# A Perceiver stack: quantised feed-forward by tiles, expert rows turned one tile ahead, one more expert tile by way of DRAM

## The chip, the cores and the metric

The kernel runs on one core of a Trainium2 chip (trn2). The metric is device time in microseconds for one execution. Three runs of the kernel before took 2646.3, 2650.88 and 2655.88 us, median 2650.88.

## What is computed

The reference is a stack of four Perceiver layers on `x` of 2 x 256 tokens by 256, with a context of 2 x 4096 by 256. Each layer has a cross-attention or a convolution over the context, an attention or state-space block, and a feed-forward; each is added to `x` after a layer norm. All is fp32 but for the layers quantised by definition. Three feed-forwards matter here.

Layer 0, a ternary-weight feed-forward with activations rounded to 8 bits:

```python
def _act_quant(x):
    scale = 127.0 / jnp.clip(jnp.max(jnp.abs(x), axis=-1, keepdims=True), 1e-05)
    xq = jnp.clip(jnp.round(x * scale), -128.0, 127.0) / scale
    return x + jax.lax.stop_gradient(xq - x)
def _bitlinear(x, w):
    return jnp.einsum('bsi,oi->bso', _act_quant(x), _weight_quant(w))
gate = jax.nn.silu(_bitlinear(x, w_gate))      # 256 -> 1024
up = _bitlinear(x, w_up)
return _bitlinear(gate * up, w_down)           # 1024 -> 256
```

Layer 2, a shared SwiGLU expert and the two best of eight SwiGLU experts (256 -> 512 -> 256) for each token, weighted:

```python
topw, topi = jax.lax.top_k(probs, TOP_K)       # of 8, TOP_K = 2
topw = jax.nn.softmax(topw, axis=-1)
eout = jnp.einsum('etf,efd->etd', jax.nn.silu(gate) * up, e_down)
spec = jnp.einsum('etd,te->td', eout, combine)
```

Layer 3, the best of eight ReLU experts (256 -> 1024 -> 256) for each token:

```python
top1 = jnp.argmax(logits, axis=-1)
for e in range(n_experts):
    h = jax.nn.relu(xf @ w1[e].T + b1[e])
    y = h @ w2[e].T + b2[e]
    out = out + jnp.where((top1 == e)[:, None], y, 0)
```

## The kernel before

The 512 tokens are NT = 4 tiles of 128 rows, one row to a partition; KC = 2 is the number of 128-wide chunks of the 256 features. The layers run one after the other. Matmuls all go through the helper `mm` (line 358). PSUM banks are dealt out in rotation under three names, `mm`, `tr` and `acc` (3, 3 and 2 banks in the stages told of here). A framework schedules the instructions and sets the semaphores; `in_order` (line 337) pins the order in which the engines named take the instructions written inside it, to the order of the text.

**Layer-0 feed-forward** (`l0_ffn`, line 908). Everything is done for all four tiles before the next step begins. `act_quant` (line 892) takes the row maxima of a whole tensor in one instruction (L896), forms the step and its inverse in four small ones (L897 to L901), and rounds each tile in three passes on DVE: scale and add ROUND (12582912, which leaves a rounded integer in the low bits, L903), subtract ROUND and clip below (L904), clip above (L905). `to_T` (line 426) turns the result on PE (L434) and copies the banks to bf16 by turns on ACT (L330) and DVE (L332). For each tile t and each half j of the 1024 hidden columns, PE makes the gate and up products, ACT the SiLU (L929), DVE the product with the up half (L930) into `h`. Then `h` is rounded as a whole by `act_quant`, turned by `to_T`, and multiplied by the down weights; L941 scales and adds the residual.

**Experts** (`l2_ffn`, line 1671, and `l3_ffn`, line 2391). Tokens are sorted by expert into n tiles of 128 rows (15 in layer 2, 11 in layer 3), each tile of one expert. The sorted rows are written to DRAM by eight (layer 3: four) indirect DMAs (L1867) and loaded back as `rows` (L1877). One unit j is one tile. Its `front` loads the expert's weights by number (`of_expert`, line 2012, on the SP queue, three buffers to each weight), turns its 128 rows (`turn_chosen` for the first tiles, straight from the tokens, `turn_rows`, line 2030, for the rest: two transposes L2033, then on DVE L2041 in layer 2, L2038 in layer 3), makes the hidden products and their nonlinearity (L1737 on ACT and L1738 on DVE in layer 2; L2447 on DVE and L2445 on ACT by turns in layer 3). Its `back` multiplies by the down weights and copies the answer (`keep_rows`, line 2043, L2045 on ACT).

Answers return to the tokens in two ways. Tiles under `kept` (11 in layer 2, 9 in layer 3) are written to DRAM `ys` by the ACT queue (L2048); when unit kept-1 has written, `fetch_rows` (line 2002) gathers each token's row by indirect DMAs of GpSimd (L2006), eight in layer 2, four in layer 3; `add` adds them, weighted, at the end (L1785, L2469). The other tiles come back by matmul: `ways_back` (line 1922) builds for each a one-hot weighted matrix `way` (L1939 and L1942 on DVE, L1943 on GpSimd; layer 3 L1936), after turning the row numbers and weights once with `on_all` (L1917, L1919), and `bring_back` (line 1946) multiplies and adds it (L1952).

`experts_in_turn` (line 1964) sets the order: front(j), then back(j-1), then the bring-back of an earlier tile if one waits, then two steps of `ways`. From unit 3 on the order of PE, DVE and ACT is pinned by `in_order`:

```python
for j in range(straight, kept):
    got = unit(j)[0]()
    back_of(j - 1, waiting)
    waiting = got
    for _ in range(2):
        next(ways, None)
```

Of the kernel before, what the change touches and what calls it, by code (L numbers as in the profile page):

```python
# [11 lines left out]
F32 = mybir.dt.float32  # L12
BF16 = mybir.dt.bfloat16
# [255 lines left out]
class Perceiver:  # L269
# [619 lines left out]
            self.ternary[name] = q, mean  # L889
            yield  # L890

    def act_quant(self, x):

        nc = self.nc
        step = self.sm.tile([P, NT], F32, name="step", tag="step")
        nc.vector.tensor_reduce(step, x, AX.X, ALU.max, apply_absolute_value=True)  # L896
        nc.vector.tensor_scalar_max(step, step, 1e-5)  # L897
        inv = self.sm.tile([P, NT], F32, name="sinv", tag="sinv")
        nc.vector.reciprocal(inv, step)
        nc.vector.tensor_scalar_mul(inv, inv, 127.0)  # L900
        nc.vector.tensor_scalar_mul(step, step, 1.0 / 127.0)  # L901
        for t in range(NT):
            nc.vector.tensor_scalar(x[:, t, :], x[:, t, :], inv[:, t : t + 1], ROUND, ALU.mult, ALU.add)  # L903
            nc.vector.tensor_scalar(x[:, t, :], x[:, t, :], ROUND, -128.0, ALU.subtract, ALU.max)  # L904
            nc.vector.tensor_scalar_min(x[:, t, :], x[:, t, :], 127.0)  # L905
        return step

    def l0_ffn(self, x):
        nc = self.nc
        with self.tc.tile_pool(name="l0f", bufs=1) as pool, self.tc.tile_pool(name="l0f2", bufs=3) as p2:  # L910
            wg, mg = self.ternary["l0f_wg"]
            wu, mu = self.ternary["l0f_wu"]
            wd, md = self.ternary["l0f_wd"]
            xn = self.layernorm(x)
            sx = self.act_quant(xn)

            xT = self.to_T(xn, pool, "xqT", dtype=BF16)
            sg = self.sm.tile([P, NT], F32, name="sg", tag="sg")
            nc.vector.tensor_scalar_mul(sg, sx, mg)
            su = self.sm.tile([P, NT], F32, name="su", tag="su")  # L920
            nc.vector.tensor_scalar_mul(su, sx, mu)
            h = pool.tile([P, NT, 1024], F32, name="h")
            for t in range(NT):
                for j in range(2):
                    pg, pu = self.bank([P, 512]), self.bank([P, 512])
                    self.mm(pg, [(xT[:, k, ts(t, P)], wg[:, k, ts(j, 512)]) for k in range(KC)])
                    self.mm(pu, [(xT[:, k, ts(t, P)], wu[:, k, ts(j, 512)]) for k in range(KC)])
                    g = p2.tile([P, 512], F32, name="gate")
                    nc.scalar.activation(g, pg, AF.Silu, scale=sg[:, t : t + 1])  # L929
                    nc.vector.scalar_tensor_tensor(  # L930
                        h[:, t, ts(j, 512)], pu, su[:, t : t + 1], g, ALU.mult, ALU.mult
                    )
            sh = self.act_quant(h)
            hT = self.to_T(h, pool, "hqT", dtype=BF16)
            sd = self.sm.tile([P, NT], F32, name="sd", tag="sd")
            nc.vector.tensor_scalar_mul(sd, sh, md)
            y = self.xp.tile([P, NT, D], F32, name="xres", tag="xres")
            for t in range(NT):
                ps = self.bank([P, D])
                self.mm(ps, [(hT[:, k, ts(t, P)], wd[:, k, :]) for k in range(8)])  # L940
                nc.vector.scalar_tensor_tensor(y[:, t, :], ps, sd[:, t : t + 1], x[:, t, :], ALU.mult, ALU.add)  # L941
            return y


# [726 lines left out]
    def l2_ffn(self, x):  # L1671
        nc = self.nc
        T = NT * P
        with ExitStack() as s:
# [17 lines left out]
            router = self.weight("l2f_router")  # L1692
            ids = pool.tile([P, 8], F32, name="ids")
            nc.gpsimd.iota(ids, [[1, 8]], base=0, channel_multiplier=0, allow_small_or_imprecise_dtypes=True)
            n, straight, kept = 15, 2, 11
            xs = self.cleared_rows(pool, n)
            along, below = self.places(pool, n)
            lg = self.bank([P, NT, 8])
# [52 lines left out]
            ys = self.rows_in_dram("ys", kept)  # L1751

            def unit(j):
                def front():
                    gu, down = self.of_expert(pool, experts, j, ("l2f_gu", 1), ("l2f_down", 1))
                    hT = p3.tile([P, KC, P], F32, name="rowsT", tag="rowsT")
                    if j < straight:
                        self.turn_chosen(pool, hT, h2, ats, along, j, "norm2")
                    else:
                        self.turn_rows(hT, rows, j, "norm2")  # L1760
                    return expert(gu, down, hT, P, "e"), down

                def back(got):
                    aT, down = got
                    ps = self.acc([P, D])
                    self.mm(ps, [(aT[:, c, :], down[:, c, :]) for c in range(4)])
                    return self.keep_rows(p3, ys, j, ps, kept)

                return front, back

            held = [self.held(pool, i, at, kept) for i, at in enumerate(ats)]

# [191 lines left out]
    def experts_in_turn(self, unit, n, kept, gather, ways, way, y):  # L1964


        e = mybir.EngineType
        done = []

        def back_of(j, got):  # L1970
            one = unit(j)[1](got)
            while done:
                at, answers = done.pop(0)
                self.bring_back(y, way[at], answers)
            if one is not None:
                done.append((j, one))

        waiting, straight = None, 3
        for j in range(straight):
            got = unit(j)[0]()  # L1980
            if waiting is not None:
                back_of(j - 1, waiting)
            waiting = got
        with self.in_order(e.PE, e.DVE, e.Activation):
            for j in range(straight, kept):
                got = unit(j)[0]()
                back_of(j - 1, waiting)
                waiting = got
                for _ in range(2):
                    next(ways, None)  # L1990
            for j in range(kept, n):
                got = unit(j)[0]()
                back_of(j - 1, waiting)
                if j == kept:
                    add = gather()
                waiting = got
            back_of(n - 1, waiting)
            add()
            at, answers = done.pop(0)
            self.bring_back(y, way[at], answers)  # L2000

    def fetch_rows(self, pool, slots, ys):
        got = [pool.tile([P, NT, D], F32, name="got", tag="got", bufs=2) for _ in slots]
        for t in range(NT):
            for g, slot in zip(got, slots):
                self.nc.gpsimd.indirect_dma_start(  # L2006
                    out=g[:, t, :], out_offset=None,
                    in_=ys, in_offset=bass.IndirectOffsetOnAxis(ap=slot[:, t : t + 1], axis=0),
                )
        return got  # L2010
# [380 lines left out]
    def l3_ffn(self, x):  # L2391
        nc = self.nc
        with self.tc.tile_pool(name="l3f", bufs=1) as pool, self.tc.tile_pool(name="l3f3", bufs=3) as p3:
# [32 lines left out]
            ys = self.rows_in_dram("ys", kept)  # L2426

            def unit(j):
                def front():
                    w1, w2 = self.of_expert(pool, experts, j, ("l3f_w1", 0), ("l3f_w2", 0))  # L2430
                    bias = w1[:, KC * 1024 :]
                    w1 = w1[:, : KC * 1024].rearrange("p (k n) -> p k n", k=KC)
                    rT = p3.tile([P, KC, P], F32, name="rowsT", tag="rowsT")
                    if j < straight:
                        self.turn_chosen(pool, rT, xn, ats, along, j)
                    else:
                        self.turn_rows(rT, rows, j)
                    hT = p3.tile([P, 8, P], F32, name="hT", tag="hT")
# [19 lines left out]
                return front, back  # L2458

            yes, slot = self.held(pool, 0, ats[0], kept)  # L2460
            way = {}
# [94 lines left out]
```

## Time and profile before

The profiled execution took 2652.49 us. Times are microseconds from the start of its span; the clock is the granted share of TensorE's full clock.

| What | Value |
|---|---|
| profiled execution | 2652.49 us |
| its span, first to last instruction | 2650.7 us |
| mean granted clock | 0.953 |
| layer-0 feed-forward: first maximum (L896) to end of the last residual add (L941) | 224.0 to 262.6 |
| layer-2 experts: first front to the end of the last add (L1952) | 1825.1 to 1938.2 |
| time from one front to the next, units 9 to 12 of layer 2 | 6.26 to 6.27 us |
| layer-3 experts: first front to the end of the last add (L1952) | 2553.2 to 2646.8 |
| time from one front to the next, units 5 to 9 of layer 3 | 8.03 to 8.05 us |
| DMA share and rate in layer 2, 1851 to 1901 | 0.76, 264 GB/s |
| DMA share and rate in layer 3, 2558 to 2573 | 1.02, 411 GB/s |

A row of the timeline gives start, duration, engine (PE matmul, PEld its weight load, DVE, ACT, POOL for GpSimd, SPq and ACTq for DMA issues), line, operation, `out<-in`, shape and count, and in brackets the engine's idle time before it and what ended that. Where rows of one operation follow each other they stand as one, with a count. An fp32 matmul has two records to one instruction of the program.

### The profile page before, as it was taken

The page shows a single profiled execution, that of the slowest core. Times are in us where ns is not written, and L with a number is a line of the kernel's source. Part 1 is how long each engine was busy: PE and PEld are TensorE (multiplying, and loading weights), DVE is VectorE, ACT ScalarE, POOL GpSimd, SP SyncE. Part 2 cuts the span into 40 slices and gives each one's busy share as a digit, 9 for nine tenths or more (in the row PEclk, how much of TensorE's full clock was granted, in tenths as well). Part 3 has the DMA queues.
Part 4 walks back from the last instruction along what each step waited for, and adds up shares of the span by engine and source line. Part 5 has one row for each costly group of instructions (what it writes and reads, how often), then busy time and mean ns, then how long its engine had stood idle before and what let it go on. Part 6 is the DMA issues. An engine that isn't in the chain of part 4 may idle for free. (4 is left out here: it accounts for less than half of the span.)

```text
span 2650.7 us, 45617 instructions
## 1 busy us (share of the span) xinstructions
PE 2498.6 (94%) x17708; PEld 1668.9 (63%) x17709; DVE 1720.2 (65%) x3191; ACT 1346.6 (51%) x2545; POOL 921.6 (35%) x865
## 2 busy tenths in 40 slices
PE   8986999999999999999899988899889999999888
PEld 6853566666666676676533555557745666665677
DVE  5566577777777777777669655444257888854632
ACT  3323566666666666666466322332115777783512
POOL 0520155555565555566549322001100222210010
PEclk9987999999999999999899998789999999998889
DMA  6210322222242222222300100006631000003565
GB/s 257 84 56 19 119 69 68 65 67 70 65 119 81 65 64 72 64 67 80 117 18 1 64 20 24 1 25 251 231 113 40 2 2 2 2 2 141 196 239 191
DMA packets 77111, 214.11 MB, mean 81 GB/s; under 512 B 6392, under 2 KB 21312, under 8 KB 66400
## 3 DMA queue, kind: packets, MB, share of 16 engines
q1 hardware_dynamic: 72128, 202.69, 23.1%
q0 software_dynamic: 1888, 5.90, 0.7%
q8 instruction: 139, 2.28, 0.3%
q10 hardware_dynamic: 2880, 2.62, 0.3%
q14 instruction: 76, 0.62, 0.1%
HBM read 190.48 MB, written 20.71 MB: 80 GB/s over the span
## 5 line engine op out<-in xcount | busy, mean ns | idle before, releaser
L1059 POOL TENSOR_TENSOR total<-total,S 128x512 f32<-128x512 f32 x434 | 541.3, 1279 | 299.3 <-ACT S L1048 298.9
L1048 ACT ACTIVATE S<-S 128x512 f32<-128x512 f32 x512 | 302.2, 625 | 209.1 <-DVE S L1045 208.9
L2145 DVE TENSOR_REDUCE mx<-ps_mm 128x1 f32<-128x512 f32 x512 | 317.9, 684 | 70.7 <-PE ps_tr L2169 53.9
L1034 DVE TENSOR_TENSOR most<-ps_mm,most 128x512 f32<-128x512 f32 x448 | 278.3, 684 | 119.2 <-ACT S L1031 119.2
L1031 ACT COPY S<-ps_mm 128x512 f32<-128x512 f32 x512 | 263.0, 599 | 116.7 <-PE ps_mm L1024 115.4
L1045 DVE TENSOR_TENSOR S<-S,ps_dec 128x512 f32<-128x512 f32 x512 | 317.6, 680 | 1.3 <-PE ps_dec L1103 1.3
L2173 ACT ACTIVATE PT<-ps_tr 128x512 f32<-128x512 f32 x476 | 246.7, 602 | 74.2 <-PE ps_tr L2169 71.7
L358 PEld LDWEIGHTS ps_tr<-w_l1x_wv,ctxT 128*128 128x128 f32 x2048 | 246.9, 192 | 52.5 <-issue 52.2
L1024 PE MATMUL ps_mm<-qT,kT 64*128 64x256 f32 x2048 | 257.1, 391 | 0.0
L358 PE MATMUL ps_tr<-ctxT,w_l1x_wk 128*128 128x512 f32 x512 | 251.8, 615 | 0.0
L1071 PE MATMUL acc<-S,v 128*64 128x256 f32 x2048 | 250.1, 385 | 0.5 <-DVE rec L1109 0.4
L358 PE MATMUL ps_tr<-w_l1x_wv,ctxT 128*128 128x128 f32 x2048 | 249.9, 275 | 0.0
L2141 PE MATMUL ps_mm<-kT,qT 32*128 32x512 f32 x1024 | 249.7, 617 | 0.2 <-DVE mx L2145 0.2
L2169 PE MATMUL ps_tr<-qm,kT 32*128 32x256 f32 x1904 | 238.2, 388 | 0.0
L1024 PEld LDWEIGHTS ps_mm<-qT,kT 64*128 64x128 f32 x2048 | 188.3, 187 | 38.9 <-DVE most L1034 3.8
L1071 PEld LDWEIGHTS acc<-S,v 128*64 128x64 f32 x2048 | 136.3, 136 | 97.1 <-ACT S L1031 38.8
L2169 PEld LDWEIGHTS ps_tr<-qm,kT 32*128 32x128 f32 x1904 | 170.8, 184 | 15.7 <-issue 6.2
L2194 POOL TENSOR_TENSOR sums<-sums,part 128x256 f32<-128x256 f32 x102 | 73.8, 724 | 257.0 <-ACT part L2193 254.2
L358 PEld LDWEIGHTS ps_tr<-ctxT,w_l1x_wk 128*128 128x128 f32 x512 | 89.7, 190 | 101.4 <-issue 100.0
L335 DVE COPY v<-ps_tr 128x512 f32<-128x512 f32 x120 | 82.9, 691 | 89.0 <-PE ps_tr L358 88.9
L2185 PE MATMUL ps_tr<-PT,v 128*32 128x256 f32 x2048 | 139.4, 385 | 0.0
L2141 PEld LDWEIGHTS ps_mm<-kT,qT 32*128 32x128 f32 x1024 | 86.1, 184 | 60.6 <-issue 48.8
(544 smaller groups left out, 3840.3 us busy)
## 6 DMA issues: line engine op xcount, KB each, us to landing
ctxT<-in_ctxT SPq DMA_DIRECT2D x144, 512.0 KB, 3.6
ctxT<-in_ctxT SPq DMA_DIRECT2D x16, 1024.0 KB, 7.7
w_l2f_gu<-in_l2f_gu SPq DMA_DIRECT2D x16, 1024.0 KB, 7.0
bd_dram<-bd SPq DMA_DIRECT2D x8, 1536.0 KB
w_l3f_w<-in_l3f_w SPq DMA_DIRECT2D x11, 1028.0 KB, 10.8
w_l3f_w<-in_l3f_w SPq DMA_DIRECT2D x11, 1024.0 KB, 5.1
ctx<-in_ctx SPq DMA_DIRECT2D x8, 1024.0 KB, 4.6
w_l2f_down<-in_l2f_down SPq DMA_DIRECT2D x16, 512.0 KB, 4.4
```

What stands on the lines that cost most here:

```text
L358: self.nc.tensor.matmul(out, lhsT, rhs, start=i == 0, stop=i == len(pairs) - 1)
L1024: nc.tensor.matmul(banks[hh, i][:, j, :], k[part, ts(2 * i + j, P)], q[u][part, :], start=True, stop=True)
L1031: nc.scalar.copy(t, ps)
L1034: nc.vector.tensor_tensor(m, ps, m, ALU.max)
L1045: nc.vector.tensor_tensor(t, t, spread[u][:, hh, :].unsqueeze(1).to_broadcast([P, 2, L]), ALU.add)
L1048: nc.scalar.activation(t, t, AF.Exp)
L1059: nc.gpsimd.tensor_add(tot, tot, t)
L1071: nc.tensor.matmul(av[u][part], vs[:, 2 * i + j, part], got[hh, i][:, j, :], start=g % 8 == 0 and i + j == 0, stop=g % 8 == 7 and i + j == 2,)
L2141: nc.tensor.matmul(ps, qT[rows, 2 * half + c, ts(t, P)], kT[rows, ts(j, 512)], start=True, stop=True,)
L2145: nc.vector.tensor_reduce(mx[:, c, r, j : j + 1], ps, AX.X, ALU.max)
L2169: nc.tensor.matmul(ps[:, i, :], kT[rows, ts(2 * u + i, P)], q[rows], start=True, stop=True)
L2173: nc.scalar.activation(pt, ps, AF.Exp, scale=0.25)
```

## The change

- `act_quant` works on any number of tiles, has three small steps instead of four, and rounds in one pass only: it leaves value plus ROUND in the tensor. A new `whole` takes ROUND away, clips above and casts to bf16 in the copy out of PSUM after the turning, always on DVE. The clip below is gone.
- `l0_ffn` goes tile by tile under `in_order`: the hidden products of tile t (`hidden`, the body of the old loop unchanged), its rounding, the turning of tile t-1, the down product of tile t-2 (now in the `acc` banks).
- A unit has three parts: `turned` is split off `front`. In `experts_in_turn` the rows of tile j+1 are turned between front(j) and back(j-1). The two pinned loops become one.
- In layer 2 `kept` goes from 11 to 12; in layer 3 it stays 9.
- `fetch_rows` gathers all tiles of the first choice, then those of the second; before, both choices of one tile, tile after tile.

```diff
-    def act_quant(self, x):
+    def act_quant(self, x, step):
...
         nc.vector.tensor_reduce(step, x, AX.X, ALU.max, apply_absolute_value=True)
-        nc.vector.tensor_scalar_max(step, step, 1e-5)
...
+        nc.vector.tensor_scalar(step, step, 1e-5, 1.0 / 127.0, ALU.max, ALU.mult)
+        inv = self.sm.tile([P, n], F32, name="sinv", tag=f"sinv{n}")
         nc.vector.reciprocal(inv, step)
-        nc.vector.tensor_scalar_mul(inv, inv, 127.0)
-        nc.vector.tensor_scalar_mul(step, step, 1.0 / 127.0)
-        for t in range(NT):
+        for t in range(n):
             nc.vector.tensor_scalar(x[:, t, :], x[:, t, :], inv[:, t : t + 1], ROUND, ALU.mult, ALU.add)
-            nc.vector.tensor_scalar(x[:, t, :], x[:, t, :], ROUND, -128.0, ALU.subtract, ALU.max)
-            nc.vector.tensor_scalar_min(x[:, t, :], x[:, t, :], 127.0)
-        return step
+
+    def whole(self, out, ps):
+
+        self.nc.vector.tensor_scalar(out, ps, ROUND + 127.0, ROUND, ALU.min, ALU.subtract)
...
+            def turned(c):
+                ps = self.bank([P, NT * P], "tr")
+                for t in range(NT):
+                    nc.tensor.transpose(ps[:, ts(t, P)], xn[:, t, ts(c, P)], self.ident)
+                self.whole(xT[:, c, :], ps)
...
+            def hidden_turned(t):
+                for i in range(2):
+                    ps = self.bank([P, 4, P], "tr")
+                    for k in range(4):
+                        nc.tensor.transpose(ps[:, k, :], h[:, t, ts(4 * i + k, P)], self.ident)
+                    self.whole(hT[:, t, ts(i, 4), :], ps)
+
+            def last(t):
+                ps = self.acc([P, D])
+                self.mm(ps, [(hT[:, t, k, :], wd[:, k, :]) for k in range(8)])
+                nc.vector.scalar_tensor_tensor(y[:, t, :], ps, sd[t], x[:, t, :], ALU.mult, ALU.add)
+
+            e = mybir.EngineType
+            with self.in_order(e.PE, e.DVE, e.Activation):
...
+                turned(0)
+                turned(1)
+                for t in range(NT + 2):
+                    if t < NT:
+                        hidden(t, 0)
+                        hidden(t, 1)
+                        self.act_quant(h[:, t : t + 1, :], sh[t])
+                        nc.vector.tensor_scalar_mul(sd[t], sh[t], md)
+                    if 0 <= t - 1 < NT:
+                        hidden_turned(t - 1)
+                    if 0 <= t - 2:
+                        last(t - 2)
...
-            n, straight, kept = 15, 2, 11
+            n, straight, kept = 15, 2, 12
...
         with self.in_order(e.PE, e.DVE, e.Activation):
-            for j in range(straight, kept):
-                got = unit(j)[0]()
-                back_of(j - 1, waiting)
-                waiting = got
-                for _ in range(2):
-                    next(ways, None)
-            for j in range(kept, n):
-                got = unit(j)[0]()
+            rowsT = unit(straight)[0]()
+            for j in range(straight, n):
+                got = unit(j)[1](rowsT)
+
+                if j + 1 < n:
+                    rowsT = unit(j + 1)[0]()
                 back_of(j - 1, waiting)
                 if j == kept:
                     add = gather()
                 waiting = got
+                if j < kept:
+                    for _ in range(2):
+                        next(ways, None)
             back_of(n - 1, waiting)
             add()
...
-        for t in range(NT):
-            for g, slot in zip(got, slots):
+        for g, slot in zip(got, slots):
+            for t in range(NT):
                 self.nc.gpsimd.indirect_dma_start(
```

More of the change, by code (lines that the diff above doesn't have):

```diff
@@ L890, in rounded @@
             yield
-    def act_quant(self, x):
-        nc = self.nc
-        step = self.sm.tile([P, NT], F32, name="step", tag="step")
+    def act_quant(self, x, step):
+        nc, n = self.nc, x.shape[1]
         nc.vector.tensor_reduce(step, x, AX.X, ALU.max, apply_absolute_value=True)
-        nc.vector.tensor_scalar_max(step, step, 1e-5)
-        inv = self.sm.tile([P, NT], F32, name="sinv", tag="sinv")
+        nc.vector.tensor_scalar(step, step, 1e-5, 1.0 / 127.0, ALU.max, ALU.mult)
+        inv = self.sm.tile([P, n], F32, name="sinv", tag=f"sinv{n}")
         nc.vector.reciprocal(inv, step)
-        nc.vector.tensor_scalar_mul(inv, inv, 127.0)
-        nc.vector.tensor_scalar_mul(step, step, 1.0 / 127.0)
-        for t in range(NT):
+        for t in range(n):
             nc.vector.tensor_scalar(x[:, t, :], x[:, t, :], inv[:, t : t + 1], ROUND, ALU.mult, ALU.add)
-            nc.vector.tensor_scalar(x[:, t, :], x[:, t, :], ROUND, -128.0, ALU.subtract, ALU.max)
-            nc.vector.tensor_scalar_min(x[:, t, :], x[:, t, :], 127.0)
-        return step
+    def whole(self, out, ps):
+        self.nc.vector.tensor_scalar(out, ps, ROUND + 127.0, ROUND, ALU.min, ALU.subtract)
     def l0_ffn(self, x):
@@ L914, in l0_ffn @@
             xn = self.layernorm(x)
-            sx = self.act_quant(xn)
-            xT = self.to_T(xn, pool, "xqT", dtype=BF16)
+            sx = self.sm.tile([P, NT], F32, name="step", tag="step")
+            self.act_quant(xn, sx)
+            xT = pool.tile([P, KC, NT * P], BF16, name="xqT")
             sg = self.sm.tile([P, NT], F32, name="sg", tag="sg")
-            nc.vector.tensor_scalar_mul(sg, sx, mg)
             su = self.sm.tile([P, NT], F32, name="su", tag="su")
-            nc.vector.tensor_scalar_mul(su, sx, mu)
@@ L922, in l0_ffn @@
             h = pool.tile([P, NT, 1024], F32, name="h")
-            for t in range(NT):
[L924 to L936, printed above, removed]
-            y = self.xp.tile([P, NT, D], F32, name="xres", tag="xres")
[L938 to L941, printed above, removed]
+            hT = pool.tile([P, NT, 8, P], BF16, name="hqT")
@@ new lines, in l0_ffn @@
+            sh = [self.sm.tile([P, 1], F32, name="hstep", tag="hstep") for _ in range(NT)]
+            sd = [self.sm.tile([P, 1], F32, name="sd", tag="sd") for _ in range(NT)]
+            y = self.xp.tile([P, NT, D], F32, name="xres", tag="xres")
+            def turned(c):
[3 more added lines that the diff above has]
+                self.whole(xT[:, c, :], ps)
@@ new lines, in hidden @@
+            def hidden(t, j):
+                pg, pu = self.bank([P, 512]), self.bank([P, 512])
+                self.mm(pg, [(xT[:, k, ts(t, P)], wg[:, k, ts(j, 512)]) for k in range(KC)])
+                self.mm(pu, [(xT[:, k, ts(t, P)], wu[:, k, ts(j, 512)]) for k in range(KC)])
+                g = p2.tile([P, 512], F32, name="gate")
+                nc.scalar.activation(g, pg, AF.Silu, scale=sg[:, t : t + 1])
+                nc.vector.scalar_tensor_tensor(h[:, t, ts(j, 512)], pu, su[:, t : t + 1], g, ALU.mult, ALU.mult)
@@ new lines, in l0_ffn @@
+            e = mybir.EngineType
+            with self.in_order(e.PE, e.DVE, e.Activation):
+                nc.vector.tensor_scalar_mul(sg, sx, mg)
+                nc.vector.tensor_scalar_mul(su, sx, mu)
+                turned(0)
[10 more added lines that the diff above has]
+                        last(t - 2)
@@ L1753, in unit, with turned @@
             def unit(j):
-                def front():
-                    gu, down = self.of_expert(pool, experts, j, ("l2f_gu", 1), ("l2f_down", 1))
+                def turned():
                     hT = p3.tile([P, KC, P], F32, name="rowsT", tag="rowsT")
@@ L1760, in front @@
                         self.turn_rows(hT, rows, j, "norm2")
+                    return hT
+                def front(hT):
+                    gu, down = self.of_expert(pool, experts, j, ("l2f_gu", 1), ("l2f_down", 1))
                     return expert(gu, down, hT, P, "e"), down
@@ L1767, in back @@
                     return self.keep_rows(p3, ys, j, ps, kept)
-                return front, back
+                return turned, front, back
             held = [self.held(pool, i, at, kept) for i, at in enumerate(ats)]
@@ L1970, in back_of @@
         def back_of(j, got):
-            one = unit(j)[1](got)
+            one = unit(j)[2](got)
             while done:
@@ L1979, in experts_in_turn @@
         for j in range(straight):
-            got = unit(j)[0]()
+            got = unit(j)[1](unit(j)[0]())
             if waiting is not None:
@@ L1984, in experts_in_turn @@
         with self.in_order(e.PE, e.DVE, e.Activation):
-            for j in range(straight, kept):
-                got = unit(j)[0]()
-                back_of(j - 1, waiting)
-                waiting = got
-                for _ in range(2):
-                    next(ways, None)
-            for j in range(kept, n):
-                got = unit(j)[0]()
+            rowsT = unit(straight)[0]()
[3 more added lines that the diff above has]
+                    rowsT = unit(j + 1)[0]()
                 back_of(j - 1, waiting)
@@ L2003, in fetch_rows @@
         got = [pool.tile([P, NT, D], F32, name="got", tag="got", bufs=2) for _ in slots]
-        for t in range(NT):
-            for g, slot in zip(got, slots):
+        for g, slot in zip(got, slots):
+            for t in range(NT):
                 self.nc.gpsimd.indirect_dma_start(
@@ L2428, in unit, with turned @@
             def unit(j):
[L2429 to L2432, printed above, removed]
+                def turned():
                     rT = p3.tile([P, KC, P], F32, name="rowsT", tag="rowsT")
@@ L2437, in front @@
                         self.turn_rows(rT, rows, j)
+                    return rT
+                def front(rT):
+                    w1, w2 = self.of_expert(pool, experts, j, ("l3f_w1", 0), ("l3f_w2", 0))
+                    bias = w1[:, KC * 1024 :]
+                    w1 = w1[:, : KC * 1024].rearrange("p (k n) -> p k n", k=KC)
                     hT = p3.tile([P, 8, P], F32, name="hT", tag="hT")
@@ L2456, in back @@
                     return self.keep_rows(p3, ys, j, ps, kept)
-                return front, back
+                return turned, front, back
             yes, slot = self.held(pool, 0, ats[0], kept)
```

## The prediction

> **What bounds the kernel now.** I read the page first. Its span is 2650.7 us; the profiled execution took 2652.49 us, so 1.8 us lie around the span, and the median of the three runs is 2650.88, 1.6 us under that execution. The engine shares:
>
> ```profile
> PE 2498.6 (94%) x17708; PEld 1668.9 (63%) x17709; DVE 1720.2 (65%) x3191; ACT 1346.6 (51%) x2545; POOL 921.6 (35%) x865
> ```
>
> PE is busy nearly throughout and carries the chain that ended last, but an average says nothing of the three stages touched, so I read each in the timeline: the layer-0 feed-forward (224 to 263 us), the layer-2 experts (1825 to 1938) and the layer-3 experts (2546 to 2647).
>
> The layer-0 stage, columns start us, duration us, engine, line, tiles, then idle time before and its releaser:
>
> ```profile
> 239.14 1.64 DVE L930 SCALAR_TENSOR_TENSOR h<-ps_mm,su,gate 128x512 f32<-128x512 f32 x2 [0.51 <-ACT gate L929]
> ...
> 240.82 4.42 DVE L896 TENSOR_REDUCE step<-h 128x4 f32<-128x4096 f32 x1
> ...
> 248.43 1.29 DVE L905 TENSOR_SCALAR h<-h 128x1024 f32<-128x1024 f32 x2
> ...
> 249.17 1.72 PE L434 MATMUL ps_tr<-ident,h 128*128 128x128 f32 x6 [9.42 <-DVE h L905]
> ...
> 252.90 1.54 PE L434 MATMUL ps_tr<-ident,h 128*128 128x128 f32 x6 [2.02 <-DVE h L905]
> ```
>
> See a serial stage: PE stands still 9.42 us while DVE takes the maxima of all four tiles and rounds in three passes, and DVE before that waited for ACT. The last residual add (L941) ends at 262.6.
>
> One layer-2 unit:
>
> ```profile
> 1885.79 1.89 PE L358 MATMUL acc<-w_l2f_down,aTe 128*128 128x256 f32 x8
> ...
> 1886.04 0.69 DVE L1738 TENSOR_TENSOR aTe<-ps_tr,gate 128x512 f32<-128x512 f32 x1 [3.76 <-issue]
> ...
> 1887.30 0.36 PEld L2033 LDWEIGHTS ps_tr<-ident,rows 128*128 128x128 f32 x2
> 1887.51 0.38 PE L2033 MATMUL ps_tr<-ident,rows 128*128 128x128 f32 x2
> ...
> 1887.93 0.61 DVE L2041 TENSOR_SCALAR rowsT<-ps_tr,cols 128x128 f32<-128x128 f32 x2 [1.20 <-PE ps_tr L2033]
> ...
> 1888.34 2.09 PE L358 MATMUL ps_mm<-rowsT,w_l2f_gu 128*128 128x128 f32 x16 [0.45 <-DVE rowsT L2041]
> ```
>
> Here PE alone sets the pace, at the full granted clock, and its only hole is from turning a tile's rows to their eviction. Layer 3 has the same hole, wider:
>
> ```profile
> 2589.75 0.38 PE L2033 MATMUL ps_tr<-ident,rows 128*128 128x128 f32 x2
> ...
> 2590.17 0.42 DVE L2038 COPY rowsT<-ps_tr 128x256 f32<-128x256 f32 x1 [2.14 <-PE ps_tr L2033]
> ...
> 2590.65 3.84 PE L358 MATMUL ps_mm<-rowsT,w_l3f_w 128*128 128x128 f32 x32 [0.52 <-DVE rowsT L2038]
> ```
>
> And one odd place, under the eight gathers of layer 2:
>
> ```profile
> 1912.57 1.03 PE L358 MATMUL acc<-y_rows,way 128*128 128x256 f32 x4
> ...
> 1914.13 0.95 POOL L2006 DMA_INDIRECT got<-ys,held_slot  x1 [0.30 <-issue]
> ...
> 1916.77 0.37 ACT L2045 COPY y_rows<-acc 128x256 f32<-128x256 f32 x1 [6.92 <-remote]
> 1916.83 0.69 DVE L1952 TENSOR_TENSOR xres<-acc,xres 128x512 f32<-128x512 f32 x1 [2.23 <-remote]
> ...
> 1917.20 2.07 PE L358 MATMUL acc<-y_rows,way 128*128 128x256 f32 x4 [3.60 <-ACT y_rows L2045]
> ```
>
> ACT's copy needs a matmul group recorded as ending at 1912.73, but the trace's semaphore events count it at 1916.75, as the last gather lands (1916.9); the group before, ended at 1911.0, is counted at 1913.84.
>
> **Layer 0.** Removed on DVE: eight 128x256 and eight 128x1024 rounding passes (L904, L905; 8 x 0.29 + 8 x 0.69 = 7.8 us). Moved to DVE: five PSUM casts from ACT (each 0.69 on DVE, 0.59 on ACT), +3.5. The new cast is a two-step tensor_scalar out of PSUM, not in the trace; nearest row is the DVE cast of the same shape, 0.69. A form at half that rate would add 10 x 0.69 = 6.9 us; one at the rate of the passes that stay in SBUF (0.69 for 1024) would save 10 x 0.34 = 3.4. I take 0.69, since L1738 and L930, which also read PSUM, cost 0.69 to 0.75 for 512.
>
> Head: quantising xn ends at 226.7 instead of 228.5; eight transposes at the half clock of this stretch (0.22 each) and two casts in a row on DVE put the first complete hidden product at about 229.2 and the first L930 at 230.3 instead of 232.09. Loop: DVE per tile is two L930 (1.4), a 128x1024 maximum (1.2, as L896 on xn), two small steps (0.4), one rounding pass (0.75), sd (0.1), two casts (1.3), one L941 (0.45): 5.6 us. PE per tile at full clock is 8 products of 0.22, 8 transposes of 0.19 and 8 products of 0.11: 4.1 us, so DVE is the bound. The order pinned for PE puts the transposes of tile t behind the products of t+1, so what queues behind that wait is only last(t-1) and the products of t+2, needed 4 us later. Tile 0 is slower, since PE is still at half clock (second L930 1.5 later): its rounding ends at 235.0. Then 5.2 + 5.65 + 4.3 bring tile 3's rounding to about 250.1; last(1), two casts, the down product (0.9) and the last L941 end near 254.9. Gain 262.6 - 254.9 = 7.7; I take 7.5. The following layernorm and the ctxT loads hang on the same last add and matmul, and move with them.
>
> [...] The profile's row for 244 to 254 agrees (granted 0.50 after the long wait). PE's pauses in the new loop are at most 1.5 us per tile[...]. By that reading PE takes 8.2 us per tile: 228.4 + 33 + 1 = 262.4, and the gain is nil.
>
> **Layer 2.** Turning moves ahead of back(j-1) on PE and behind aTe(j) on DVE. PE per unit becomes 3.71 (front, 1882.08 to 1885.79) + 0.22 (two transposes) + 1.72 (back) = 5.65 for 6.27. The eviction ends about 1.5 us after the front, inside the 1.94 until the next front: it is hidden by back(j-1); without that cover it costs the old 0.62. The moved transposes need only rows that have landed (the row load's packets end at 1837), and bank turns older than a unit. Unit 4 gains 0.55 (the on_all transposes stay exposed), units 5 to 12 gain 8 x 0.62: 5.5 us by front(12), 1895.4 for 1900.87. The weight stream must rise from 264 to about 280 GB/s; stretches of this stage already ran at over 400. The issue of a gate/up load stands some 10 us ahead of its use against 7.0 to land.
>
> The twelfth tile: removed are four bring-back matmuls (1.72 PE), two adds (1.4 DVE) and one way tile (1.5 DVE, 1.27 POOL); added one 0.33 issue on ACT. But the gather waits for unit 11 instead of 10. It starts 5.2 us after that back (1900.0 to 1905.24 before): 1901.0 + 5.2 = 1906.2, and lands 11.6 later, 1917.8. fetch_rows' new order only means that the first add needs the fifth gather; the last landing bounds it as before.
>
> What then? [...] front(14) at 1906.65, three backs and bring-backs of 1.72 after it end at 1917.1, eight adds (L1785, 3.7 us) and two of 0.69 end at 1922.8 instead of 1938.2: 15.4. The rows above say otherwise: PE's counts came 3 to 4 us late from the fifth gather on, and by 0.9 to 1.3 us under the eight scatters (1815 to 1822), nowhere under four. Eight gathers remain, so I take the row: everything stands till 1917.8, the second half of the bring-back at half clock takes 2.1, back(14) another 1.7 too long, and from back(14) to the end it is 9.3 (1928.89 to 1938.2 before): 1930.8. Gain 7.4.
>
> **Layer 3.** front(3) still waits for its weights (1.4 ahead of 2573.05), so nothing before it moves. Unit 4 no longer waits for the way tile and on_all's copy: 2573.05 + 3.65 + 0.22 + 3.45 + 0.44 = 2580.8 for 2582.62. Units 5 to 10: 7.32 for 8.03, 6 x 0.71 = 4.3. Weights for unit 5 land at 2582.8, needed at 2588.1; later the stream needs 288 GB/s of the 420 seen. The gather after unit 8 lands about 3 us ahead of its adds. Gain 1.8 + 4.3 = 6.1, say 6.2.
>
> **Sum.** 7.5 + 7.4 + 6.2 = 21.1. Profiled: 2652.49 - 21.1 = 2631.4; 1.6 less for the median: 2629.8, so 2630.
>
> **Rivals.** First, the late counts do not return: 29.1 us, 2622; for it speaks that the place is one trace's. Second, half clock in the layer-0 loop: 13.6 us, 2637; the clock row speaks for it, PE's short pauses against. Third, the moved turning brings nothing because the weight loads become the limit and units keep 6.27 and 8.03: layer 0 and one bring-back stay, 9.2, 2642; against it speak 5 us of slack per load. Fourth, slower: in layer 0 the pinned order fails to overlap tiles. Then each tile costs products at half clock 3.4, SiLU 0.7, two L930 1.5, maximum and steps 1.6, rounding 0.75, transposes 3.4, casts 1.4, down 1.8 and add 0.5, that is 15 us, and four cost 60 against 32.7, 27.3 lost for 13.6 gained: 2650.9 + 13.7, or 2665. It decides from 11.6 us per tile, where four cost 46.3 = 32.7 + 13.6; against it speaks the order, with a whole tile between rounding and its casts.
>
> **How the numbers follow.** Forecast 0.62, counts on time 0.22, half clock 0.07, weight limit 0.07, no overlap 0.02. A measurement of this kernel tells about 0.3% (8 us) from no change; the weight case lies on that edge, 0.05 of it within. Faster 0.93, same 0.05, slower 0.02. The range, 2619 to 2641, takes in the late counts gone, the half clock, and a cast dearer by half.
>
> **What would show it.** Right: no PE idle over 3 us between 230 and 254 and no L905 left; a unit period of 5.65 in layer 2 and 7.3 in layer 3 with rowsT's wait gone; got's first gather near 1906.2 - 7.5 = 1898.7, and a "remote" wait at its end. Wrong: granted clock 0.5 through the layer-0 loop, DMA named before a front, casts over 1 us.

## The result and the profile after

The changed kernel took 2613.69, 2616.86, 2620.25 and 2625.09 us, median 2618.56, beside 2649.75 for four runs of the kernel before: a ratio of 0.9885, 95% interval 0.9862 to 0.9908, or 31 us (24 to 37). Forecast were 2630 and 2619 to 2641: the sign held, and the mechanism but for one term of layer 2; the median lies just under the range, and 20.9 us of gain had been worked out where 31 came. The profiled execution took 2616.86 us with a span of 2615.1, which is 35.6 us under that of before, and goes by stages so (a stage as in the table of before):

| Stretch | Before | After | Gain | Forecast |
|---|---|---|---|---|
| start to the first maximum of layer 0 | 224.0 | 225.1 | -1.2 | 0 |
| layer-0 feed-forward | 38.6 | 31.5 | 7.1 | 7.5 |
| from there to the first front of layer 2, not touched | 1562.5 | 1553.0 | 9.5 | 0 |
| layer-2 experts | 113.2 | 98.55 | 14.6 | 7.4 |
| from there to the first front of layer 3, not touched | 614.9 | 616.1 | -1.2 | 0 |
| layer-3 experts | 93.7 | 86.9 | 6.8 | 6.2 |

So the three stages gave 28.5 us for the 21.1 forecast, nearly all of the difference in layer 2, and 7.1 more came from code that the change leaves alone. The page's engine row shows how little an average tells of that: PE is busy for 18.6 us less, DVE for 6.7.

```profile
PE 2480.0 (95%) x17701; PEld 1659.1 (63%) x17701; DVE 1713.5 (66%) x3184; ACT 1343.4 (51%) x2540; POOL 919.3 (35%) x864
```

Layer 0 in the timeline of the changed kernel:

```profile
230.81 1.28 ACT L938 ACT_TABLE_LOAD   x1 [7.32 <-PE ps_mm L358]
...
232.82 1.47 DVE L939 SCALAR_TENSOR_TENSOR h<-ps_mm,su,gate 128x512 f32<-128x512 f32 x2 [2.75 <-ACT gate L938]
...
245.69 1.28 DVE L905 TENSOR_SCALAR hqT<-ps_tr 128x512 bf16<-128x512 f32 x2
...
251.45 1.56 PE L945 MATMUL ps_tr<-ident,h 128*128 128x128 f32 x8 [3.49 <-DVE sd L964]
...
252.81 3.34 PE L358 MATMUL acc<-q_l0f_wd,hqT 128*128 128x256 bf16 x16
```

The 9.42 us of PE's idle time are gone; its waits are for DVE (sd is the last step of a tile's rounding), and two casts take 1.28 us, 0.68 each with their overlap, for the 0.69 assumed. Two things are not as forecast: SiLU's table is loaded only when the first product is there, and the last two down products run at half clock (granted 0.50 from 252.3 to 255.7; 3.34 us for sixteen matmuls, where the eight of the tile before had taken 1.04), after an idle time of 3.49 ahead of the last tile's transposes. That is over the 3 us that the prediction had named as its limit.

One unit of layer 2, and one of layer 3:

```profile
1876.75 0.38 PE L2064 MATMUL ps_tr<-ident,rows 128*128 128x128 f32 x2
1876.97 1.89 PE L358 MATMUL acc<-w_l2f_down,aTe 128*128 128x256 f32 x8
...
1877.62 0.60 DVE L2072 TENSOR_SCALAR rowsT<-ps_tr,cols 128x128 f32<-128x128 f32 x2
1878.70 1.95 PE L358 MATMUL ps_mm<-rowsT,w_l2f_gu 128*128 128x128 f32 x16
```

```profile
2573.58 3.73 PE L358 MATMUL ps_mm<-rowsT,w_l3f_w 128*128 128x128 f32 x32
...
2578.41 0.41 DVE L2069 COPY rowsT<-ps_tr 128x256 f32<-128x256 f32 x1
...
2580.83 3.40 PE L358 MATMUL ps_mm<-rowsT,w_l3f_w 128*128 128x128 f32 x29
```

No PE row has a bracket: the view marks no wait of PE. The eviction of rowsT ends 0.5 us (layer 3: 2.0) ahead of its use, under the down product. A unit takes 5.52 us in layer 2 (1873.18 to 1878.70) and 7.25 in layer 3. That is under the 5.65 and 7.32 forecast, because the sixteen matmuls that open a front had cost 2.09 behind a wait and cost 1.95 without one (32: 3.84 and 3.73).

The end of layer 2, where the forecast had everything standing until the last gather lands:

```profile
1898.68 1.03 PE L358 MATMUL acc<-y_rows,way 128*128 128x256 f32 x4
...
1900.63 0.37 ACT L2076 COPY y_rows<-acc 128x256 f32<-128x256 f32 x1 [5.02 <-PE acc L358]
...
1902.05 1.29 DVE L1982 TENSOR_TENSOR xres<-acc,xres 128x512 f32<-128x512 f32 x2 [4.39 <-remote]
...
1903.25 3.75 DVE L1815 SCALAR_TENSOR_TENSOR xres<-got,part,xres 128x256 f32<-128x256 f32 x8
```

The counts of PE's groups are late here too: the last back and half a bring-back, which ended at 1898.84 and 1899.70, are counted at 1900.61 and 1902.02, as the last gather lands (1902.2). That is what ACT's 5.02 and DVE's 4.39 of idle time end with. But the last front is long over, and only the last copy and the adds wait.

### The profile page after: what moved, and what is told of

The parts are those of the page before. It is cut to its first block, busy times and chain, and to the rows that moved or that the text cites. A ratio compares the mean times of both kernels' runs of the same rounds, so it can differ in the third digit from the quotient of the medians.

```text
span 2615.1 us, 45590 instructions
## 1 busy us (share of the span) xinstructions
PE 2480.0 (95%) x17701; PEld 1659.1 (63%) x17701; DVE 1713.5 (66%) x3184; ACT 1343.4 (51%) x2540; POOL 919.3 (35%) x864
## 4 chain that ended last, share of the span: by engine, by line
PE 39%; DVE 6%; issue 2%; ACT 2%; POOL 2%; DMA 0%; another core or an unknown queue 0%; DVEq 0%; ACTq 0%; POOLq 0%; SPq 0%
PE ps_mm L358 10%; PE ps_mm L2172 5%; PE ps_tr L2216 5%; PE ps_tr L2200 4%; PE ps_tr L358 3%; PE acc L358 3%; PE ps_mm L785 2%; DVE state L1357 1%; POOL spread L1345 1%; PE ps_tr L2335 1%; PE acc L826 1%; PE ps_tr L801 1%; PE ps_tr L2378 1%; PE ps_mm L2360 1%; PE acc L1583 1%
## 5 line engine op out<-in xcount | busy, mean ns | idle before, releaser
L1051 PE MATMUL ps_mm<-qT,kT 64*128 64x256 f32 x2048 | 255.7, 389 | 0.0
```

What stands on the lines that cost most here:

```text
L1051: nc.tensor.matmul(banks[hh, i][:, j, :], k[part, ts(2 * i + j, P)], q[u][part, :], start=True, stop=True)
```

## The experiments

Three questions: do the parts add up; where do the 9.5 us of an untouched stretch come from; and what are the late counts (PE's matmul groups counted by their semaphore after they had ended) worth, and what do they go with? Runs told under one chip ran on it side by side, with runs of the kernel before; there were three chips (that of the first pair of profiles is not recorded). All runs have a profile; totals are medians of timed runs, but for the three that are called single executions.

**The parts (first chip; the kernel before took 2645.14 us there).** The layer-0 part alone:

```diff
-            sh = self.act_quant(h)
-            hT = self.to_T(h, pool, "hqT", dtype=BF16)
...
+                    if t < NT:
+                        hidden(t, 0)
+                        hidden(t, 1)
+                        self.act_quant(h[:, t : t + 1, :], sh[t])
...
```

> Layer-0 part alone, experts as before. Theory: the stage from the first maximum to the last residual add lasts 31 to 32.5 us instead of 38.6, the layer-2 and layer-3 stages stay within 1 us of 113.1 and 93.6; total 2650 - 7 = 2643. For the 9.5 us that the changed kernel won between the end of layer 0 and the first layer-2 front, in code that the change leaves alone: if they are chance of the clock windows, that stretch lies anywhere from 1553 to 1563 here and the total stays near 2643; if the shorter layer 0 brings them (a shift of phase, or PE at full clock when it ends), the stretch is 1553 here too and the total near 2633.

Measured: 2635.55 us, ratio 0.9963 (0.995 to 0.9976), 10 us (6 to 13). The layer-0 stage lasts 31.46 us; the untouched stretch 1556.1, which lies where chance may put it and not at the 1553 of the rival. What nobody expected: the layer-2 stage, whose code is that of before, lasts 107.04 us and not 113.2.

Turning a tile ahead alone (kept stays 11, the old order of gathers, the old layer 0):

```diff
+            rowsT = unit(straight)[0]()
+            for j in range(straight, n):
+                got = unit(j)[1](rowsT)
+                if j + 1 < n:
+                    rowsT = unit(j + 1)[0]()
                 back_of(j - 1, waiting)
```

> Turning a tile ahead alone, eleven kept tiles, old order of the gathers, old layer 0. Theory: units of 5.5 to 5.65 in layer 2 and 7.25 in layer 3; layer 3 gains 6.2 to 6.8. In layer 2 the gather of eleven tiles starts a unit earlier than in the changed kernel; if late PE counts are a matter of eight gathers alone, PE stands again in the middle of the tail and layer 2 gains only about 5.5 (107.6 long); if the stall is gone anyway once units are shorter, layer 2 gains 12 or more (101 or less). Total 2638 or 2631. The untouched stretch before layer 2: 1562 if layer 0 brings its gain, 1553 to 1563 if it is chance.

Measured: 2630.85 us, ratio 0.9947 (0.9933 to 0.9961), 14 us. Layer 2 lasts 98.24 us, layer 3 87.59; the untouched stretch 1555.9 with the old layer 0. Against 107.04 and 93.78 of the run before on the same chip this part is worth 8.8 and 6.2 us.

Twelve kept tiles alone:

```diff
-            n, straight, kept = 15, 2, 11
+            n, straight, kept = 15, 2, 12
```

> Twelve kept tiles alone, all else as before. Theory that the lateness costs nothing once it falls on the last gather, which the adds await anyway: layer 2 gains 1.7 (one bring-back) plus the 6 to 7 us of stall and half clock, 104 to 106 long, total about 2642. Rival, late counts cost the same wherever the gather lies: gain 1.7 to 2, 111 long, total 2648.

Measured: 2643.65 us, ratio 0.9992 (0.9982 to 1.0003). Layer 2 lasts 104.89 us: 2.15 under the 107.04 of this chip. Both theories had set out from 113; from 107 the gain is that of one bring-back, and there was no stall to save.

Both together, still with the old layer 0 and the old order of gathers:

```diff
-            n, straight, kept = 15, 2, 11
+            n, straight, kept = 15, 2, 12
...
+                if j + 1 < n:
+                    rowsT = unit(j + 1)[0]()
```

> The experts' part without layer 0 and with the old order of the gathers (both choices of one tile, tile after tile). Theory: the order of the gathers is worth nothing, since all adds wait for the last landing: layer 2 lasts 98 to 99.5, layer 3 86.8, total 2650 - 14.6 - 6.8 = 2628.6. Rival: the new order is what lets PE's counts come in time; then layer 2 lasts 103 to 106 and the total is about 2635.

Measured: 2631.10 us, ratio 0.9942 (0.9921 to 0.9963), 15 us. Layer 2 lasts 96.51 us, layer 3 86.89. So the parts add up: 8.8 for turning ahead and 1.7 for the twelfth tile in layer 2, 6.9 in layer 3, 7.1 in layer 0, 24.5 us on this chip. That is by the lengths of the stages: the two totals, 2630.85 and 2631.10, do not tell the twelfth tile. In none of the four traces is a PE group counted late under the gathers.

**The same two kernels once more (second chip; 2649.76 us).** Unchanged code:

```diff
 (no edit: the kernel before, and the changed kernel)
```

> The kernel before once more, unchanged. Theory: PE's late counts under the gathers of layer 2, and the half clock after them, were a matter of that one execution; this one shows the layer-2 stage in 107.0 us (as the layer-0 part alone did, whose expert code is that of before) and no PE group counted late. Rival: they belong to this program, and the stage lasts 111 to 113 us again. The stretch between layer 0 and layer 2 lasts 1552 to 1563 us, by 0.42 us for every us of half clock in it.

> The changed kernel once more, unchanged. Theory: layer-0 stage 31.5 us, layer 2 in 96.5 us (as with the old order of the gathers, if that order is worth nothing) and without late counts, layer 3 in 86.9; against an undisturbed execution of the kernel before that makes 7.1 + 10.5 + 6.8 = 24.4 us, a ratio of 0.9908; total about 2621. Rival: the 98.55 us of the first profile are the price of the new order of the gathers, and return.

Measured: 2650.93 us for the kernel before. The changed kernel took 2620.10 us, ratio 0.9890 (0.9876 to 0.9905), 29 us (25 to 33). The theory that the late counts were one execution's accident fell: the layer-2 stage lasts 114.90 and 98.58 us, with groups counted late in both. What did turn out to be accident is the untouched stretch. These are the rows of busy time of the two repeats, before first, each from the last layer-0 add to the first layer-2 front (start and end, length, busy time of PE, of its weight loads, of DVE, ACT and POOL, granted clock, DMA share, GB/s):

```profile
264.70:1817.20 1552.50, 1491.52 (x9057) 966.38 (x9058) 1083.75 (x1895) 848.29 (x1530) 758.06 (x647) 0.97 0.21 65
```

```profile
256.00:1815.50 1559.50, 1498.24 (x9057) 968.88 (x9057) 1084.02 (x1896) 848.24 (x1530) 757.84 (x647) 0.96 0.21 64
```

The order is turned round: the changed kernel takes 7 us more there than that of before. DVE, ACT and POOL do the same work to 1 us in these two and in the first pair; PE's busy time moves with the length (1501.74 us in 1562.4 and 1492.15 in 1553.0 in the first pair). By the granted clock's record the stretch holds 105.8 and 122.9 us at half rate (129.7 and 109.2 in the first pair), and over all 14 profiles of this study (105.8 to 129.7 us at half rate, 1552.5 to 1562.5 long) each such microsecond goes with 0.42 us more of the stretch, with a correlation of 0.98 and no point more than 1.0 us off the line.

**Layer 0: what sets its pace (second chip).** Every second cast of hqT on ACT, without the clip above:

```diff
-                    self.whole(hT[:, t, ts(i, 4), :], ps)
+                    self.whole(hT[:, t, ts(i, 4), :], ps, less if i else None)
...
+        if less is not None:
+            self.nc.scalar.activation(out, ps, AF.Identity, bias=less)
+            return
```

> The changed kernel with every second cast of hqT on ACT instead of DVE (that half without the clip above). Theory that DVE sets the pace of the layer-0 loop: DVE has 0.65 us less per tile, so the maxima of tiles 2 and 3 come 0.65 and 1.3 us earlier and the stage lasts 29.6 to 30.3 us instead of 31.5. Rival, that PE or ACT sets it (PE waits, clock, gates): 31.3 or more.

Measured: stage 28.38 us, total 2621.72 us, ratio 0.9897 (0.9883 to 0.9912). In its timeline, at the same place:

```profile
249.41 1.09 PE L950 MATMUL ps_tr<-ident,h 128*128 128x128 f32 x8 [3.09 <-DVE h L901]
...
250.34 1.91 PE L358 MATMUL acc<-q_l0f_wd,hqT 128*128 128x256 bf16 x16
```

DVE is the bound: its last rounding ends 1.2 us earlier from the stage's start. The rest of the 3.1 us comes from the end, where the sixteen down matmuls run at full clock (granted 1.00 from 247.8 to 254.6), 1.91 for 3.34.

One small SiLU ahead of the loop, which brings its table in early:

```diff
                 nc.vector.tensor_scalar_mul(su, sx, mu)
+                early = pool.tile([P, NT], F32, name="early")
+                nc.scalar.activation(early, sg, AF.Silu)
                 turned(0)
```

> The changed kernel with one small SiLU on ACT ahead of the layer-0 loop, so that the 1.28 us of its table are loaded while DVE still rounds. Theory that the table load is what put the first product h 2.5 us later than forecast: first L939 1.28 us earlier after the first maximum, and 0.6 to 1.3 us off the stage (30.2 to 30.9). Rival, that PE at half clock sets the head: no change in the second L939 and 31.5.

Measured: stage 30.68 us, total 2622.38 us, ratio 0.9904 (0.989 to 0.9918):

```profile
225.79 1.28 ACT L958 ACT_TABLE_LOAD   x1 [3.56 <-DVE sg L955]
...
230.34 0.75 DVE L939 SCALAR_TENSOR_TENSOR h<-ps_mm,su,gate 128x512 f32<-128x512 f32 x1 [1.53 <-PE ps_mm L358]
```

The first product h comes 6.45 us after the first maximum instead of 7.68, and DVE now waits for PE: the table was the head's delay, and 0.8 us of it reach the end.

**What do the late counts go with? (third chip; 2647.95 us).** So far they were in both first profiles and on the second chip in every kernel, and nowhere on the first. The kernel before and the layer-0 part alone, unchanged, side by side:

```diff
 (no edit: the kernel before, and the layer-0 part alone)
```

> The kernel before a third time, beside the layer-0 part alone on the same chip (next run). The four kernels that showed no late counts ran on one chip, those that did on another, and the code of the experts does not tell them apart. Theory, lateness goes with the chip: this run and the next agree, both with a layer-2 stage of 107.0 us and no PE group counted late, or both with 111 to 115 us and late counts. Rival, it goes with the program: 113 to 115 us here and 107.0 in the next.

> The layer-0 part alone once more, experts as before. Lateness goes with the chip: layer-2 stage as in the run before this one, within 3 us. Lateness goes with the program: 107.0 us whatever the run before shows. Layer-0 stage 31.5 us.

Measured (a single execution each): 2647.63 and 2639.84 us; the layer-2 stage lasts 113.34 and 113.12. The layer-0 part alone is one program on two chips, so its rows can be laid side by side, first chip, then third:

```profile
1900.18 1.89 PE L358 MATMUL acc<-y_rows,way 128*128 128x256 f32 x8
1900.38 0.37 ACT L2072 COPY y_rows<-acc 128x256 f32<-128x256 f32 x1 [2.92 <-PE acc L358]
...
1903.11 2.09 PE L358 MATMUL ps_mm<-rowsT,w_l2f_gu 128*128 128x128 f32 x16 [0.83 <-DVE rowsT L2068]
```

```profile
1899.02 1.03 PE L358 MATMUL acc<-y_rows,way 128*128 128x256 f32 x4
...
1903.13 0.37 ACT L2072 COPY y_rows<-acc 128x256 f32<-128x256 f32 x1 [6.83 <-remote]
...
1903.55 2.07 PE L358 MATMUL acc<-y_rows,way 128*128 128x256 f32 x4 [3.51 <-ACT y_rows L2072]
...
1906.67 3.46 PE L358 MATMUL ps_mm<-rowsT,w_l2f_gu 128*128 128x128 f32 x16 [0.61 <-DVE rowsT L2068]
```

On the first chip the copy follows the down product at once (group ended 1900.34, counted 1900.36); on the third the same copy waits for a count that comes at 1903.11 for a group that ended at 1899.18, PE stands 3.51 us, its next four matmuls take 2.07 us for 1.03 (as at this place in the kernel before, 2.07 from 1917.2 on at a granted 0.50), and the next front takes 3.46 for 2.09. The gathers themselves are alike: first issue at 1892.86 and 1891.80, last packet at 1904.1 and 1903.1, 11.2 and 11.3 us later. So the lateness does not go with the program. It goes with the chip, or with the time at which that chip ran: each chip's runs were made together, and nothing here tells these two apart.

Half the gathers, on this chip (the kernel before; the second choice's kept rows are left out, and its adds take the first choice's):

```diff
-        got = [pool.tile([P, NT, D], F32, name="got", tag="got", bufs=2) for _ in slots]
+        got = [pool.tile([P, NT, D], F32, name="got", tag="got", bufs=2)] * len(slots)
         for t in range(NT):
-            for g, slot in zip(got, slots):
+            for g, slot in zip(got[:1], slots):
```

> The kernel before with only the four gathers of the first choice; the second choice's rows of kept tiles are left out, and the eight adds all take the first choice's rows. Theory that PE's counts come late because eight gathers follow one another: none late here, layer-2 stage 107.0 us, on a chip where the kernel before shows 111 to 115. Rival, any indirect DMA beside PE does it on such a chip: counts 1 to 4 us late under the four too, stage over 110. If the kernel before shows no lateness in this call, both give 107.0 and the run says nothing.

Measured (a single execution): the layer-2 stage lasts 107.04 us, to the hundredth that of the first chip with all eight gathers:

```profile
1820.68 0.42 DVE L1749 TENSOR_TENSOR xres<-acc,xres 128x256 f32<-128x256 f32 x1 [2.42 <-PE acc L358]
...
1911.03 1.89 PE L358 MATMUL acc<-y_rows,way 128*128 128x256 f32 x8
1911.23 0.37 ACT L2045 COPY y_rows<-acc 128x256 f32<-128x256 f32 x1 [2.92 <-PE acc L358]
```

With four in a row no count is late, and the front behind the gathers takes 2.09 us (from 1913.96), where in the kernel before on this chip it took 3.78; with eight 6.1 to 7.9 us are lost (113.1 to 114.9 less 107.04). One execution could have escaped the effect by chance, but this one had it: under its eight scatters, which the edit leaves, a group that ended at 1819.51 is counted at 1820.66, and the first row shown is the add that waited for it. All fourteen traces, read from end to end, say the same: ahead of the last two counts of the program, groups counted over 0.5 us late stand only around the eight scatters and the eight gathers of layer 2, in all ten traces that are not of the first chip, and never around four in a row, here or in layer 3. That the total is 2647.30 us all the same comes from stretches that the edit leaves alone: layer 0 began 3.7 us later than in the kernel before, and it, the untouched stretch and the one behind layer 2 took another 2.8 more together.

Last, both layer-0 edits in one:

```diff
+                nc.scalar.activation(early, sg, AF.Silu)
...
+                    self.whole(hT[:, t, ts(i, 4), :], ps, less if i else None)
```

> The changed kernel with every second cast of hqT on ACT and the early SiLU. The two were worth 3.1 and 0.8 us of the layer-0 stage by themselves; if they add up, it lasts 27.6 us, if the head and the loop share a wait, 28.4. Layers 2 and 3 as in the changed kernel. Total 3.9 us under the changed kernel, 0.9875 of before.

Measured: stage 30.03 us and not 27.6; total 2623.98 us, ratio 0.9911 (0.9894 to 0.9927), no better than the changed kernel's 0.9890. Its busy time by window, and that of the ACT cast alone, columns as above:

```profile
243.70:247.10 3.40, 1.32 (x13) 0.96 (x10) 3.37 (x8) 0.69 (x1) 0.00 (x0) 1.00 0.01 2
247.10:250.50 3.40, 2.39 (x11) 2.16 (x12) 3.05 (x7) 0.39 (x1) 0.00 (x0) 0.50 0.00 0
```

```profile
244.40:247.80 3.40, 1.92 (x16) 1.56 (x16) 3.40 (x7) 0.69 (x1) 0.00 (x0) 1.00 0.01 2
247.80:251.20 3.40, 1.79 (x16) 1.69 (x17) 3.33 (x10) 0.66 (x1) 0.00 (x0) 1.00 0.00 0
```

The changed kernel, for comparison, has at this place:

```profile
248.90:252.30 3.40, 0.85 (x6) 0.64 (x7) 3.33 (x9) 0.00 (x0) 0.00 (x0) 1.00 0.00 0
252.30:255.70 3.40, 3.40 (x18) 2.47 (x17) 3.33 (x8) 0.00 (x0) 0.00 (x0) 0.50 0.00 0
```

The first two kernels have the same wait of 3.09 us ahead of the last tile's transposes. In the one with both edits it leaves PE 1.32 us of work in a window, and the clock is 0.50 from then to 253.9; in the other it falls across a boundary, with 1.92 and 1.79 us on its sides, and the clock stays at 1.00 to the stage's end. The 2.4 us missing from the forecast 27.6 are this half clock: eight transposes take 1.97 us for 1.09, sixteen down matmuls 3.62 for 1.91. No version of layer 0 can be told from the changed kernel by its total.

## Why the prediction was nearly right

- **Layer 0, 7.5: right by its mechanism, by its number partly by luck** (7.1 here, 7.4 to 7.9 in the pairs of the other two chips). DVE sets the pace, as moving a cast off it shows; the clock stays full through the loop (granted 1.00 from 233.5 to 252.2), so the half-clock rival, an estimate of 8.2 us of PE per tile, fell, and the no-overlap rival with it. That pauses of 1.5 us would leave the clock full was the author's estimate too. Inside the sum several terms were off and nearly cancelled. The head was 1.3 us too short: the table load stands behind a PE wait, and the trace of before had hidden it; 0.5 of it was left at the end of tile 0's rounding, whose second product came 0.7 us after the first and not 1.5. Tiles 1, 2 and 3 took 3.9, 5.1 and 5.65 us for 5.2, 5.65 and 4.3: no casts come ahead of tile 1 yet, and they do ahead of tile 3. The end was 0.6 too short, because "pauses at most 1.5 us per tile" doesn't hold for the last tile, when PE has nothing else: 3.49 idle, and down products at half clock.
- **Layer 2, 7.4: mechanism right, and the term for the late counts mis-sized.** By front 12 the units gained 6.8 us for the 5.5 forecast, since a front without a wait is 0.14 us shorter. The gather started 81.0 us after the first front (forecast 81.2) and landed at 92.5 (92.8). The step that failed is "I take the row: everything stands till 1917.8", which charged 8.0 us (15.4 less 7.4) to late counts. They did return, but cost 2.0 (98.55 here for 96.51 on the chip without them, where the gathers had the old order). The groups held back were only the last back and the bring-backs, where in the kernel before a whole front and two backs were still to come behind them, and no half clock followed (granted 1.00 through the stage, 0.96 before). From the landing to the end it took 6.0 us, two adds of a bring-back, the eight and two more, and not 13. The rival "counts on time" named 15.4 and is near by its number; its premise, that the counts would be on time, was the author's assumption and is false where this was profiled. Its sum also leaves out one of the five groups of 1.72 that follow front(14) (1906.65 + 3.71 + 5 x 1.72 = 1919.0 for 1917.1), which changes nothing, since the adds behind the landing end later. In shares: 8.8 turning ahead, 1.7 the twelfth tile, 4.1 from lateness that costs 2.0 in place of 6.1; together 14.6.
- **Layer 3, 6.2: right** (6.8 here; 6.2 to 6.9 in the others), the rest being the shorter front. The weight stream was no limit in either layer, with no wait of PE for weights from 1812 to 1900 or from 2580 to 2610 (252 GB/s through the layer-2 stage, a DMA share of 0.73): that rival fell.
- **Nothing elsewhere: right for the change, not for one pair of profiles.** The 9.5 us of the untouched stretch go with its half-clock time, and in the repeat the sign turned. The repeat's own stages (7.9 + 16.3 + 6.4 = 30.6) agree with its timed 29 us (25 to 33); without late counts it would be 24.5, if the parts of the first chip are added (the changed kernel itself was not run there).

What stays open: why late counts come on two chips and not on a third, and what is held up, PE's count, its delivery, or the group itself (the ends of matmuls in these traces are modelled); the trace shows only when the count arrives. The new order of the gathers was not run by itself; the adds ran unbroken (3.74 and 3.75 us) with either.

## What to carry to other kernels

Put a price on a stall that one profile shows only after a second profile of the same kernel: here the stage that seemed to last 113 us lasted 107 on another chip, and a stretch of unchanged code moved by 10 us. When a transfer or a late signal can't be avoided, move it to where only its own consumer is left: with the late counts at the very end of layer 2 they cost 2 us, with a front behind them 6 to 8. Work moved one tile ahead can gain more than the wait that it removes: here the sixteen matmuls behind a wait of 0.45 took 2.09 us, and 1.95 without it.

## What the runs showed of the hardware

- PE's groups were counted late under eight gathers in a row, on two of three chips, and not under four on one of these two: by 1.8 and 2.3 us in the changed kernel, by 2.8 to 4.0 in the kernel before, and by up to 4.2 in its repeat (a group that ended at 1904.89 let ACT copy at 1909.14). On the first chip the count came 0.02 us after the group's end (1900.34 and 1900.36). What is late is a signal: the down product itself took 1.89 us in the changed kernel both before the first gather (from 1888.01) and between the gathers (from 1893.31).
- Half clock comes in steps of 3.4 us: in each of the fourteen traces all changes of the granted clock fall on one grid of 3.413 us (59 changes before and 55 after, none more than 0.03 us off it). In the three tables of windows above, windows with 0.85 and 1.32 us of PE work were followed by half clock, those with 1.79 and 1.92 were not. The same wait of 3.09 us cost the clock or not by where it fell. Over the windows of all fourteen traces, half clock followed every one of the 178 at full clock with less than 1.4 us of PE work, but also 136 of the 542 with 2.0 to 2.8: the busy time of PE is not all that decides, and what else does is open.
- A cast of 128x512 out of PSUM to bf16 took 0.68 us on DVE with two operations (0.69 for the two of xqT), and 0.69 on ACT with a bias: neither form was dearer than the plain DVE cast of before (0.69); ACT's plain cast had taken 0.59.
